# Turning the output projection of an attention kernel round, so that it yields the transposed result by seven block products

## The chip, the core and the metric

The kernel runs on one core of a Trainium2 chip. The core has a matrix engine (TensorE, "PE" in the profile, its weight loads "PEld"), a vector engine (VectorE, "DVE"), an engine for functions of one operand (ScalarE, "ACT"), a general engine (GpSimd, "POOL") and a queue processor (SyncE, "SP") that issues most of the DMAs. TensorE writes to PSUM, eight banks of 512 float32 values in each of 128 partitions; everything else lives in SBUF or in DRAM. The metric is device time in microseconds; the median of several runs counts. A profile is one further execution with its own time.

## What is computed

Eight images of 32 x 32 pixels with 256 channels pass through two attention layers, in float32.

```python
# layer 0: four heads, no mask; n = 1024 pixels, C = 256
q, k, v = split(x @ W_qkv)                  # per head, each n x 256
p   = softmax(q @ k.T * C**-0.5)            # n x n
res = concat_heads(p @ v)                   # n x 1024
x1  = res @ W_out + b_out + x
# layer 1: one head, 32 channels for f and g
f, g, h = x1 @ Wf + bf, x1 @ Wg + bg, x1 @ Wh + bh
y = gamma * (softmax(g @ f.T) @ h) + x1     # the output
```

Layer 0 has nearly all of the work: 32 pairs of image and head, each with two 1024 x 1024 x 256 products, against one narrow and one wide product an image in layer 1.

## The kernel before

**Folding.** For each head the kernel first forms `wqk`, the product of the query weights and the transposed key weights, and `wvo`, the product of the value weights and this head's rows of `W_out`. Scores then need only x and one projected q, and the values are x itself: `y` = x^T p, unnormalised, is projected by `wvo` at the end. x is held in rows (`rows`, pixels on the partitions) and transposed (`xT`, channels on the partitions).

**Seven products.** Most matrix products of layer 0 are cut into 2 x 2 blocks and done by seven block products instead of eight. `sum_a` and `sum_b` form the four sums of blocks that each side needs, on VectorE; `seven` runs the products in three thirds, `one`, `two` and `three`, into three PSUM banks x, y and z, and forms the four result blocks by a copy on ScalarE (`e`, and block 11) and five additions on VectorE (`u`, `v`, 22, 21, 12). The queries, the scores and `y` are made so. The projection is not: `project` does four matmuls of 128 x 128 by 128 x 256 for two groups of 128 rows (`po`, line 637), with `y` as the stationary side, and adds each group to the accumulated rows `rows1` by one VectorE instruction (line 648) that multiplies by the inverse of the softmax sum, a column with one value a row.

**Steps.** The program is a list of steps, each one block of 512 columns (`blk` 0 or 1) of one head of one image; for every image after the first, the two blocks of layer 1 of the image before stand between the heads (after head 1, for the last image after head 3). A step runs the scores of its own block, the products `y` of the block one step earlier (`one`), and the projection of the block two steps earlier (`two`). The last third of `y` runs into the next step.

**Order.** Within a step `put` gives every task a place from 0 to 10, and tasks are issued by place. TensorE, VectorE and ScalarE work strictly in this order (`manual_schedule`); a task that waits holds up what stands behind it on its engine. SP and GpSimd take theirs as the program gives it. Two pools of PSUM banks serve all: `ps` with 6 banks, for scores and `y`, and `psm` with 2, for the projection, the values of layer 1 and f and g.

**The sums of p.** `sums` forms the block sums of p for `y` and, from them, the sums over rows (`keys`): a wide add, two narrower ones, a reduction over partitions on GpSimd (line 593), a DMA of the row to DRAM (`line`) and one back as a column of four per partition (`st`). `invert` takes the inverses.

**Layer 1.** x1 has to be transposed. `turn_rows` does it without TensorE: DMAs move 32 x 32 squares to their place (line 377) and `nc.vector.transpose` turns each square (lines 382, 385). For x1 the squares go through the f-and-g tile. The last image's x1 is transposed on TensorE (`transpose_rows`) in the last step. `values` projects h by row groups into `v` (one `psm` bank a task, evacuated at line 729), `queries_apart` makes f and g; layer 1's product with p is `row_products`, which adds to `rows1` and leads to the output.

Buffers that the change touches: `rows` has 4, `xT` 2; `m0`, `rs`, `rb` one each.

Of the kernel before, what the change touches and what calls it, by code (L numbers as in the profile page):

```python
# [16 lines left out]
P = 128  # L17
# [3 lines left out]
def kernel(  # L21
# [14 lines left out]
):  # L36

# [111 lines left out]
    bout_sb = const.tile([P, C], F32, tag="bout", name="bout_sb")  # L149
# [8 lines left out]
    def load_rest():  # L158
        with nc.allow_non_contiguous_dma(reason="small bias vectors, loaded once"):
            nc.sync.dma_start(bout_sb, b_out.partition_broadcast(P))  # L160
# [20 lines left out]
    wblocks = {}  # L181
# [52 lines left out]
    def seven(name, width, parts, matmuls, outs, tags, copy, after=None):  # L234
# [7 lines left out]
        def bank(k):  # L242
            banks[k] = tile_of("ps", [P, NB], f"ps{k}_{name}")[:, :width]
# [22 lines left out]
        def one():  # L266
            for k, number in (("x", 1), ("y", 6), ("z", 5)):
                bank(k)
                product(k, number, True)
            nc.scalar.copy(scratch("e"), banks["x"])  # L270
            add(shaped(scratch("u")), "y", sbs["e"])
# [19 lines left out]
    NARROW = dict(e="eh", u="uh", v="w")  # L291

    def fold_weights(h):
# [20 lines left out]
        def multiply(i, what):  # L314
# [13 lines left out]
            if i == 0:  # L328
# [4 lines left out]
                wblocks[h] = b_operands(blocks, sums)  # L333

# [22 lines left out]
    def turn_rows(b, src, dst, layer, scratch=None):  # L357

        Q = 32

        def end():
            if b not in dst:
                dst[b] = tile_of("xT", [P, CC, N], f"x{layer}T_{b}")
            return dst[b]

        def flat(t):
            return t.rearrange("p u n -> p (u n)").rearrange("p (s q) -> p s q", q=P)  # L370

        def move(a, c=None):
            to, rows_v = flat(end() if scratch is None else scratch()), flat(src[b])
            if c is not None:
                to, rows_v = to[:, ts(c, NT), :], rows_v[:, c::CC, :]
            for q in range(P // Q):
                nc.sync.dma_start(to[ts(q, Q), :, ts(a, Q)], rows_v[ts(a, Q), :, ts(q, Q)])

        def piece(k, c):
            to = end()[:, c, ts(k, NB)]  # L380
            if scratch is None:
                nc.vector.transpose(to, to)
            else:
                squares = scratch()[:, k, :].rearrange("p (t c q) -> p t c q", c=CC, q=P)
                nc.vector.transpose(to.rearrange("p (t q) -> p t q", q=P), squares[:, :, c, :])

        return (
            [partial(move, a, c) for a in range(P // Q)
             for c in ((None,) if scratch else range(CC))],
            [partial(piece, k, c) for k in range(NBLK) for c in range(CC)],  # L390
        )

# [32 lines left out]
    def residual(b):  # L425


        def piece(i):
            if i == 0:
                rows1[b] = tile_of("rows", [P, NT, C], f"x1_{b}")  # L430
            nc.vector.tensor_tensor(
                rows1[b][:, ts(i, 2), :], rows[b][:, ts(i, 2), :],
                bout_sb.unsqueeze(1).broadcast_to([P, 2, C]), ALU.add,
            )

        return [partial(piece, i) for i in range(NT // 2)]
# [40 lines left out]
    def values_tile(name):  # L477
        v = tile_of("v", [P, NT, CV], name)
        nc.gpsimd.memset(v[:, :, C : C + 1], 1.0)
        return v  # L480


    class Layer0:
        def __init__(self, b, h):
            self.b, self.h, self.name = b, h, f"{b}_{h}"
            self.p, self.y, self.r = {}, {}, {}
            self.products_of, self.pblocks = {}, {}
# [8 lines left out]
        def queries(self):  # L496
# [6 lines left out]
            def after():  # L503
                t = tile_of("qs", [P, 3, NBLK, HB], f"qs_{self.name}")
                q = self.q.rearrange("p c (k e i) -> p c e k i", k=NBLK, e=2)
                blocks = [q[:, c, e] for c in range(CC) for e in range(2)]
                sums = [blocks[1]] + [t[:, k] for k in range(3)]
                self.pieces = sum_b(sums, *blocks)
                self.blocks = b_operands(blocks, sums)

            def piece(k):
                self.pieces[k]()  # L512

# [7 lines left out]
                WIDE, nc.scalar.copy, after,  # L521
            ), [partial(piece, k) for k in range(4)]

        def scores(self, blk):
# [10 lines left out]
            for g in range(0, half, 2):  # L535
# [3 lines left out]
                def after(g=g, out=out):  # L539
# [8 lines left out]
                         self.blocks[number][:, blk, :])  # L548
# [10 lines left out]
        def sums(self, blk):  # L559
# [6 lines left out]
            def start():  # L566
# [4 lines left out]
                s2 = tile_of("s2", [P, half, HB], f"s2_{n}")  # L571
                s3 = tile_of("s3", [P, half, HB], f"s3_{n}")
                sums = [t[:, 1], s2, s3, t[:, 0]]
# [8 lines left out]
            def first():  # L582
                t = made["t"]
                made["m"] = m = tile_of("m0", [P, 2, 2, HB], f"m_{n}")
                tt(m, t[:, :, 0:2, :], t[:, :, 2:4, :], ALU.add)

            def second():
                m = made["m"]
                r = tile_of("rs", [P, 2, HB], f"rs_{n}")
                tt(r, m[:, :, 0, :], m[:, :, 1, :], ALU.add)  # L590
                tt(r[:, 0, :], r[:, 0, :], r[:, 1, :], ALU.add)  # L591
                t = tile_of("rb", [P, NB], f"rb_{n}")
# [9 lines left out]
            return [partial(piece, i) for i in range(4)], [first, second]  # L602

        def invert(self, blk):
            n = self.first + blk * HT
            nc.vector.reciprocal(inverse[:, n : n + HT], self.r[blk])
# [22 lines left out]
        def project(self, blk):  # L629

            b = self.b
# [501 lines left out]
```

## Time and profile before

| | |
|---|---|
| Time, median of 3 runs | 2338.89 us (2338.29 to 2339.77) |
| The profiled execution | 2338.61 us; its span on the core 2336.7 us |
| Granted TensorE clock | 0.999 |
| VectorE, ScalarE, GpSimd busy | 1481.7, 522.5, 211.5 us |
| `po` matmuls | 1024 instructions, 128 x 128 by 128 x 256 |
| DMA | 42.94 MB, mean 18 GB/s; 158160 of 170257 packets under 512 B |

A row of a group reads: line, engine, operation, output tile <- input tiles, shapes, count | busy time in us, mean ns of one | idle time of the engine just before them, and who ended it. A float32 matmul shows as two instructions. A line of the timeline reads: start in us, length in us, engine, line, what it is, how many were merged, and in brackets the idle time of the engine before it with what ended it. A line of waits reads: who waited for whom, us in total, times, longest.

VectorE's longest rows in one ordinary step are the sums over 128 x 1024 elements (1.21 us each), the additions from PSUM of 128 x 512 (0.69 us) and of 128 x 256 (0.42 us). The reduction over partitions takes GpSimd 3.2 us a block. In the tail, the last step begins at 2248.8 us with the last third of `y` of block 0, and the span ends at 2336.7 with the last rows of layer 1 of the last image.

### The profile page before, as it was taken

Reading aid. Unit: us, or ns where it says so; the run is one execution under the profiler, and the core shown is the slowest. Engines: PE = TensorE matmul, PEld = TensorE weight load, DVE = VectorE, ACT = ScalarE, POOL = GpSimd, SP = SyncE. Lnnn points to the kernel's source line nnn. Section 1 sums busy time; section 2 is a strip of 40 time slices with the busy share of each in tenths; the row PEclk is TensorE's granted clock in tenths of the full one; section 3 lists DMA queues with packets and bytes.
Section 4 is the critical chain, followed back from the end, with each engine's and each line's share of the span. In section 5 each row is a group of like instructions: output and inputs, shape, how many; then the busy total and the mean of one; then the engine's idle time right before and its main releaser. Section 6 shows DMA issues by size and latency. Waiting matters only on the chain.

```text
span 2336.7 us, 26026 instructions
## 1 busy us (share of the span) xinstructions
PE 2326.9 (100%) x10394; PEld 1918.8 (82%) x10394; DVE 1481.7 (63%) x2398; ACT 522.5 (22%) x875; POOL 211.5 (9%) x79
## 2 busy tenths in 40 slices
PE   9999999999999999999999999999999999999999
PEld 7888888788878888788887888878888788888877
DVE  6667775377754767557774577645776457766635
ACT  2222222222221222212222122221222222222222
POOL 0111111011110111101111011110011101101110
PEclk9999999999999999999999999999999999999999
DMA  4000010100101001110011000110001100000100
GB/s 138 1 1 1 1 37 14 34 1 11 27 17 32 1 19 21 19 29 1 19 26 18 24 1 19 30 18 19 1 19 30 19 19 1 1 1 1 30 7 31
DMA packets 170257, 42.94 MB, mean 18 GB/s; under 512 B 158160, under 2 KB 163024, under 8 KB 170128
## 3 DMA queue, kind: packets, MB, share of 16 engines
q1 hardware_dynamic: 170128, 41.20, 8.0%
q8 instruction: 84, 1.38, 0.3%
q14 instruction: 45, 0.37, 0.1%
HBM read 13.37 MB, written 8.52 MB: 9 GB/s over the span
## 4 chain that ended last, share of the span: by engine, by line
PE 99%; DVE 1%; DMA 0%; issue 0%; ACT 0%
PE psy_y L247 14%; PE psy L247 14%; PE psx L247 9%; PE pa_l L834 9%; PE po L637 9%; PE psx_y L247 9%; PE psz_y L247 9%; PE psz L247 9%; PE psy_q L247 4%; PE psx_q L247 2%; PE psz_q L247 2%; PE pr_v_l L466 2%; PE ps_l L746 1%; PE pm_fg L703 1%; PE pwqk L318 0%; PE pwvo L318 0%
## 5 line engine op out<-in xcount | busy, mean ns | idle before, releaser
L593 POOL PARTITION_ALL_REDUCE rb<-rs x64 | 206.9, 3233 | 2046.6 <-DVE rs L591 2019.8
L247 PE MATMUL psx<-q,x0T 128*128 128x256 f32 x1024 | 263.6, 380 | 0.0
L247 PE MATMUL psy<-qs,xs 128*128 128x256 f32 x1024 | 263.0, 379 | 0.0
L247 PE MATMUL psz<-q,xs 128*128 128x256 f32 x1024 | 262.8, 379 | 0.0
L541 ACT ACTIVATE p<-p 128x1024 f32<-128x1024 f32 x128 | 135.3, 1057 | 554.8 <-DVE p L264 554.8
L247 PE MATMUL psy_y<-s,xt 128*128 128x256 f32 x1024 | 242.4, 380 | 0.1
L637 PE MATMUL po<-wvo,y 128*128 128x256 f32 x1024 | 241.9, 379 | 0.0
L247 PE MATMUL psx_y<-p,x 128*128 128x256 f32 x1024 | 241.9, 379 | 0.0
L834 PE MATMUL pa_l<-v_l,s_l 128*128 128x257 f32 x1024 | 232.1, 381 | 0.4 <-DVE v_l L729 0.4
L247 PEld LDWEIGHTS psx<-q,x0T 128*128 128x128 f32 x1024 | 194.0, 190 | 45.2 <-issue 21.0
L637 PEld LDWEIGHTS po<-wvo,y 128*128 128x128 f32 x1024 | 194.6, 190 | 39.5 <-issue 14.8
L834 PEld LDWEIGHTS pa_l<-v_l,s_l 128*128 128x128 f32 x1024 | 193.8, 190 | 36.6 <-issue 10.5
L247 PEld LDWEIGHTS psx_y<-p,x 128*128 128x128 f32 x1024 | 194.7, 190 | 34.0 <-issue 8.6
L247 PEld LDWEIGHTS psy_y<-s,xt 128*128 128x128 f32 x1024 | 191.9, 190 | 30.6 <-issue 2.4
L247 PEld LDWEIGHTS psy<-qs,xs 128*128 128x128 f32 x1024 | 194.5, 190 | 27.0 <-DVE qs L512 0.4
L247 PEld LDWEIGHTS psz<-q,xs 128*128 128x128 f32 x1024 | 194.7, 190 | 26.3
L264 DVE TENSOR_TENSOR u<-psy,e 128x512 f32<-128x512 f32 x128 | 88.4, 691 | 144.3 <-ACT e L270 73.4
L276 ACT ACTIVATE p<-psx 128x512 f32<-128x512 f32 x128 | 76.4, 597 | 413.7 <-PE psx L247 413.6
L264 DVE TENSOR_TENSOR v<-psy,e 128x512 f32<-128x512 f32 x128 | 87.8, 686 | 124.5 <-PE psy L247 124.5
L247 PE MATMUL psy<-qs,x0T 128*128 128x256 f32 x512 | 131.6, 380 | 0.7 <-DVE v L264 0.7
L648 DVE SCALAR_TENSOR_TENSOR x<-po,inverse,x 128x256 f32<-128x256 f32 x256 | 111.9, 478 | 31.3 <-PE po L637 22.4
L270 ACT COPY e<-psx 128x512 f32<-128x512 f32 x128 | 73.8, 576 | 257.8 <-PE psx L247 257.8
(120 smaller groups left out, 2839.8 us busy)
## 6 DMA issues: line engine op xcount, KB each, us to landing
out_dram<-x SPq DMA_DIRECT2D x15, 512.0 KB, 2.6
x<-in_x_dram SPq DMA_DIRECT2D x14, 512.0 KB, 4.6
x0T<-x SPq DMA_DIRECT2D x224, 32.0 KB, 1.9
fg<-x SPq DMA_DIRECT2D x112, 64.0 KB, 2.1
fg<-fg SPq DMA_DIRECT2D x56, 64.0 KB, 2.0
w<-in_L_conv_W_qkv_dram SPq DMA_DIRECT2D x4, 512.0 KB, 7.3
x<-in_x_dram SPq DMA_DIRECT2D x4, 256.0 KB, 4.8
w<-in_L_conv_W_qkv_dram SPq DMA_DIRECT2D x4, 256.0 KB, 6.4
```

Of the source, the lines that this page charges most:

```text
L247: nc.tensor.matmul(banks[k][:, ts(i, w)], lhsT=lhsT, rhs=rhs, start=first and n == 0, stop=True, skip_group_check=True,)
L264: nc.vector.tensor_tensor(dst, shaped(banks[k]), shaped(other), ALU.add)
L270: nc.scalar.copy(scratch("e"), banks["x"])
L276: copy(outs["11"](), shaped(banks["x"]))
L466: nc.tensor.matmul(pm[:, ts(j, C)], lhsT=src()[:, c, ts(2 * t2 + j, P)], rhs=w()[:, c, :], start=(c == 0), stop=(c == CC - 1),)
L541: exp(both, both)
L593: nc.gpsimd.partition_all_reduce(t, r.rearrange("p e i -> p (e i)"), P, bass_isa.ReduceOp.add)
L637: nc.tensor.matmul(pm[:, ts(j, C)], lhsT=self.y[blk][:, c, ts(2 * t2 + j, P)], rhs=folded[self.h][1][:, c, :], start=(c == 0), stop=(c == ...
L648: nc.vector.scalar_tensor_tensor(acc, pm[:, ts(j, C)], inverse[:, n : n + 1], acc, ALU.mult, ALU.add)
L703: nc.tensor.matmul(pm[ts(k, half)], lhsT=w[:, c, :], rhs=x1T_of[b][:, c, ts(k, NB)], start=(c == 0), stop=(c == CC - 1),)
L746: nc.tensor.matmul(pm, lhsT=self.f[ts(r, CK), ts(j0 + r, P)], rhs=self.g[ts(r, CK), ts(blk, NB)], start=True, stop=True,)
L834: nc.tensor.matmul(pm[:, : C + 1], lhsT=p[:, j, ts(ti, P)], rhs=v[:, j, : C + 1], start=(j == 0), stop=(j == NT - 1),)
```

## The change

The projection is turned round. With `wvo` stationary and `y` moving, it gives the transposed contribution, channels on the partitions, and it runs through `seven`: the four sums of `wvo` are formed once a head (`oblocks`), those of `y` in every step (`yt`). It takes two PSUM banks of the `psm` pool, since y and z share one (`two_banks`). The result `o` (in the `m0` buffer) now needs one inverse per column: the inverses, after `invert`, are written to DRAM as a row and spread to all partitions (`invb`) by two DMAs, and one VectorE instruction multiplies a step later; for the last block the inverse is taken of the reduced row itself (`invert_all`). GpSimd then issues a DMA that adds `o` to `x1T` in SBUF. `x1T` starts as x^T plus the bias (`residual`, now on ScalarE, in step 1 of the image). Layer 1 reads `x1T` directly; the rows of x1, needed for the output, come from turning `x1T` back (`turn_back`), for the last image too, so no transposition on TensorE is left there.

Around it: the sums of q are made for one block at a time; the sums of p share storage (one in place of a block of p, one in place of another sum) and their row sums are added row by row; the intermediate of f and g lies in the values' tile, which is taken earlier; x of the next image is loaded and turned one head earlier; `rows` gets 3 buffers and `xT` 3.

```diff
-    def seven(name, width, parts, matmuls, outs, tags, copy, after=None):
+    def seven(name, width, parts, matmuls, outs, tags, copy, after=None, two_banks=False):
@@
+            if not two_banks:
+                banks[k] = tile_of("ps", [P, NB], f"ps{k}_{name}")[:, :width]
+            elif k == "z":
+                banks[k] = banks["y z"][:, width : 2 * width]
+            else:
+                t = tile_of("psm", [P, NB], f"ps{k}_{name}")
+                banks["y z"], banks[k] = t, t[:, :width]
@@ fold_weights
+                t4 = const.tile([P, 4, P], F32, tag=f"wo{h}", name=f"wo{h}")
+                sums = [t4[:, k, :] for k in range(4)]
+                blocks = [t[:, c, ts(e, P)] for e in range(CC) for c in range(CC)]
+                run(sum_a(sums, *blocks))
+                oblocks[h] = a_operands(blocks, sums)
@@ residual
-            nc.vector.tensor_tensor(
-                rows1[b][:, ts(i, 2), :], rows[b][:, ts(i, 2), :],
-                bout_sb.unsqueeze(1).broadcast_to([P, 2, C]), ALU.add,
+            nc.scalar.activation(
+                x1T_of[b][:, c, :], xT_of[b][:, c, :], AF.Identity, bias=boutT_sb[:, c : c + 1]
             )
@@ sums
-                sums = [t[:, 1], s2, s3, t[:, 0]]
+                sums = [t[:, 1], t[:, 0], blocks[2], t[:, 0]]
@@
-                tt(m, t[:, :, 0:2, :], t[:, :, 2:4, :], ALU.add)
+                tt(r, t[:, :, 0, :] if k == 1 else r, t[:, :, k, :], ALU.add)
@@ invert
+            line = tile_of("line", [1, NB], f"inv_{self.name}_{blk}")
+                nc.sync.dma_start(line.rearrange("o (t p) -> p (o t)", p=P), inv)
+            self.rb[blk] = t = tile_of("invb", [P, NB], f"invb_{self.name}_{blk}")
+            nc.sync.dma_start(t, line[0].partition_broadcast(P))
@@ project
-                        nc.tensor.matmul(
-                            pm[:, ts(j, C)],
-                            lhsT=self.y[blk][:, c, ts(2 * t2 + j, P)],
-                            rhs=folded[self.h][1][:, c, :],
-                    nc.vector.scalar_tensor_tensor(
-                        acc, pm[:, ts(j, C)], inverse[:, n : n + 1], acc, ALU.mult, ALU.add
-                    )
+                    y = self.y[blk]
+                    t = tile_of("yt", [P, 3, HB], f"yt_{n}")
+                    blocks = [y[:, c, ts(e, HB)] for c in range(CC) for e in range(2)]
+                    sums = [blocks[1]] + [t[:, k] for k in range(3)]
+                    made["l"] = sum_b(sums, *blocks)
+                    made["b"] = b_operands(blocks, sums)
...
+            def add():
+                o = made["o"]
+                nc.vector.tensor_tensor(
+                    o, o, self.rb[blk].unsqueeze(1).broadcast_to([P, CC, NB]), ALU.mult
+                )
+                nc.gpsimd.dma_start(
+                    x1T_of[self.b][:, :, ts(blk, NB)], o, accum_op=ALU.add
+                )
+            return [partial(piece, i) for i in range(4)], seven(
+                f"o_{n}", HB, 1,
+                lambda number: [(0, oblocks[self.h][number], made["b"][number])],
...
+                LAST, nc.scalar.copy, two_banks=True,
+            ), [add]
@@ the steps
-            put(u.project(k), *((3, 7) if l0 else (2, 6) if blk == 0 else (3, 7)))
+            ysums, tasks, adds[i] = u.project(k)
+            put(ysums, *((1.1, 1.2, 1.3, 3.3) if l0 else (2.6, 2.7, 2.8, 3.1) if blk == 0 else
+                         (1.1, 1.2, 1.3, 2.1)))
+            put(tasks, *((3, 5.5, 7) if l0 else (5.2, 6, 7.2) if blk == 0 else
+                         (3, 5, 7) if nxt else (2.1, 4.1, 4.6)))
+        if i - 1 in adds:
+            put(adds[i - 1], 0.5)
@@
-                moves, turned = turn_rows(a.b - 1, rows1, x1T_of, 1, step(i + 2)[0].fg_tile)
-                put(moves, 0.1, 0.2, 0.3, 0.4)
-                put(turned, 5.4, 6.4, 7.2, 7.4)
+                moves, turned1 = turn_back(a.b - 1)
+                put(moves, 3, 4, 5, 6, 7, 8, 8.9, 9.3)
@@
         if not l0 and blk == 0:
             put(a.values(), 0.9, 1, 3, 5, 8)
+            put(turned1, 2.5, 2.9, 4.2, 5.1)
         if nxt is None:
-            put(transpose_rows(B - 1, rows1, x1T_of, 1), 2.5, 4.5, 8.1, 8.2)
-            put(final.queries(), 2.4, 6.5, 9)
+            fg = final.queries()
+            moves, turned1 = turn_back(B - 1)
+            put(moves, *[9.1 + 0.1 * k for k in range(8)])
@@
-    run(own[:1], s0[:1], prod[:1], p0[:1], s0[1:], prod[1:2], p0[1:2])
-    weave((prod[2:] + own[1:], 0, 1), (s1, 0.3, 0.7), (p1[:2], 0.55, 0.95), (p0[2:], 0.1, 0.9))
+    run(own[:1], prod[:1], fg, s0[:1], p0[:1], prod[1:2], s0[1:], p0[1:2])
+    weave((prod[2:] + own[1:], 0, 1), (s1, 0.3, 0.7), (p1[:2], 0.55, 0.95), (p0[2:], 0.1, 0.9), (turned1, 0.3, 1))
```

## The prediction

> **What bounds the kernel now.** I read the page first (busy shares, the chain of waits, the costliest groups), then TensorE's own waits, then the timeline of three stretches: an ordinary step of layer 0, a step with layer 1 in it, and the tail.
>
> ```profile
> PE 2326.9 (100%) x10394; PEld 1918.8 (82%) x10394; DVE 1481.7 (63%) x2398; ACT 522.5 (22%) x875; POOL 211.5 (9%) x79
> PE 99%; DVE 1%; DMA 0%; issue 0%; ACT 0%
> L637 PE MATMUL po<-wvo,y 128*128 128x256 f32 x1024 | 241.9, 379 | 0.0
> L648 DVE SCALAR_TENSOR_TENSOR x<-po,inverse,x 128x256 f32<-128x256 f32 x256 | 111.9, 478 | 31.3 <-PE po L637 22.4
> ...
> PE psy L247 <- DVE v L264: 0.7, 2, 0.3
> PE pa_l L834 <- DVE v_l L729: 0.4, 1, 0.4
> ```
>
> TensorE is the chain: 99% of it, and its waits on VectorE over the whole span are 0.7 and 0.4 us. So every matmul removed is time removed, and every wait newly put on TensorE is time added; nothing else counts. The stretch below, steps of head 0 of one image, gives the pitch and the room:
>
> ```profile
> 1121.47:1149.10 27.63, 27.63 (x130) 24.27 (x128) 19.66 (x32) 6.04 (x10) 3.41 (x3) 1.00 0.01 1
> 1149.10:1182.60 33.50, 33.50 (x143) 26.89 (x142) 25.10 (x41) 7.21 (x12) 2.98 (x2) 1.00 0.10 32
> ...
> 1129.24 1.89 PE L637 MATMUL po<-wvo,y 128*128 128x256 f32 x8
> 1130.97 1.03 PE L247 MATMUL psy<-qs,x0T 128*128 128x256 f32 x4
> 1131.83 1.03 PE L247 MATMUL psz<-q,xs 128*128 128x256 f32 x4
> ```
>
> The columns after the stretch are its length and the busy time of PE, PEld, DVE, ACT and POOL. Eight `po` instructions start 1.73 us before their successor, so one takes 0.216 us, not the 379 ns of its row, which overlap. VectorE has 8.0 and 8.4 us free in these steps, but it works in a fixed order, so where its work stands matters as much as how much there is.
>
> **What the Trainium skill says.** "Perfetto Trace Analysis", section Identifying the Most-Contended Engine: matmul busy time is a poor measure, weight-load busy a better one. Here PE shows 100% and PEld 82%; since TensorE's waits are about 1 us, I take the pitch as the bound all the same. "DMA: Bandwidth & Descriptors", section SWDGE vs HWDGE vs iDMA: accumulating during a DMA is possible only from GpSimd's queue; no run here has one. The same page, Anatomy of one DMA, prices such a DMA at 2.0 us plus bytes over 436 GB/s; the trace has only SP's transfers of 512 KB, which land in 2.6 us (output) and 4.6 us (loads). "SBUF — State Buffer", section Who interferes with whom: VectorE with two SBUF inputs contends with GpSimd's reads, not its writes, so making descriptors beside the sums should not be held; no trace here shows it.
>
> **The change part by part.**
> *TensorE, removed.* The projection of a block goes from 8 products of 256 columns to 7; each is two instructions. 64 blocks x 2 x 0.216 = 27.6 us. The 16 transposes of x1 in the last step go as well: four take 0.43 us (2263.85 to 2264.28), so 1.7 us. Together 29.3.
>
> *VectorE, added.* Per block: four sums of y (0.42 each, as L591) 1.7; five adds from PSUM (0.42, as `u_y`) 2.1; one multiplication of 128x1024 (as L580) 1.21; minus four of L648 at 0.478, 1.9. That is +3.1, times 64 = 199 us. Sums of q by block: 256 x 0.42 instead of 128 x 0.685, +20. Sums of p row by row: 3 x 0.685 + 0.425 instead of 1.215 + 0.68 + 0.425, +10. Sums of wvo 16 x 0.29 = 5, a further turned image 3; the residual (21) moves to ScalarE. VectorE comes to about 1698 us, 73%. ScalarE gets 64 x (0.357 + 0.372) + 16 x 1.06 = 64 us, reaching 25%. Totals bind nothing; order might.
>
> *Ordinary steps, hidden.* I laid out an even step of layer 0 by these durations: TensorE 27.2 us, VectorE 23.2 us. The tight points are where TensorE needs a sum: the third sum of y is ready 7.8 us into the step, wanted at 8.2; the second sum of p at 12.1, wanted at 12.5; the last add of the step ends about 1 us into the next, where the PSUM bank is wanted 1.7 us in. So nothing is lost, with 0.3 to 0.7 us to spare; if VectorE were 0.5 us later, about 0.2 us would be lost at some 45 such steps. The odd steps (33.1 us) have a little more room; head 0's, with the sums of x, is even.
>
> *Inverses and accumulation, hidden.* The row of sums takes 3.2 us on GpSimd and about 4 us through the two small DMAs; the inverse then goes to DRAM and back to all partitions, two more at about 2 us each, wanted a step (27 us) later. Ahead of it on SP stand at worst four turning DMAs of 0.69 us. The product is scaled by 4.3 us into the step after; GpSimd then issues the 512 KB accumulation. By the skill's price that is 3.2 us, an estimate; doubled for reading the destination, 6. The next user of its one buffer (`m0`) is ScalarE's copy 16.4 us into the step, so 12 us are free. Below it costs nothing, above it ScalarE's exponentials queue behind the copy and TensorE's banks behind them. I take 3 to 6.
>
> *Steps with layer 1, added.* The first third of the projection now stands right behind a values task and needs two `psm` banks; one is the bank that task has just filled. The fourth values task of one such step, and its evacuation:
>
> ```profile
> 969.32 1.89 PE L466 MATMUL pr_v_l<-wh_sb,x1T 128*128 128x256 f32 x8
> 971.04 1.89 PE L637 MATMUL po<-wvo,y 128*128 128x256 f32 x8
> ...
> 971.25 0.75 DVE L729 SCALAR_TENSOR_TENSOR v_l<-pr_v_l,gamma_sb,bh_sb 128x512 f32<-128x512 f32 x1 [1.83 <-PE pr_v_l L466]
> ```
>
> The bank is free at 972.0; the second product would start at 971.04 + 0.43 = 971.5. That is 0.55 us; the next third follows at once and waits about 0.25 for the add that reads the same bank. 0.8 x 7 images = 5.6 us. Were the evacuation queued behind one sum of p (1.2), 14; none stands there.
>
> *Tail, added.* x1 of the last image is no longer transposed on TensorE but turned by 32 DMAs and four transposes of VectorE (0.70 each) placed among the last values tasks.
>
> ```profile
> 986.77 17.16 SPq L377 DMA_DIRECT2D x0T<-x  x25
> ...
> 2305.44 0.74 DVE L729 SCALAR_TENSOR_TENSOR v_l<-pr_v_l,gamma_sb,bh_sb 128x512 f32<-128x512 f32 x1
> 2306.34 25.37 PE L834 MATMUL pa_l<-v_l,s_l 128*128 128x257 f32 x116 [0.39 <-DVE v_l L729]
> ```
>
> One DMA takes SP 17.16/25 = 0.69 us, all 32 take 22, plus 2 to land. They start once the output of the block before is written, 23 us after that step began, so end near 47; VectorE arrives at the first transpose near 45.5 and stops for about 2. Behind it stand the evacuations of the values, which already today end late enough to hold TensorE 0.39 us. The four transposes put the last of them 2.9 us later, the re-placed maxima of p add about 1: 4.1 us, or 6.3 with the stop. I take 5.3. The f and g matmuls of the last image are there before and after; their evacuation holds the first scores 0.4 us. With the two thirds placed side by side in the last step (0.6) that is 1 us more; the head of the kernel and the first image, whose turned x meets full steps, get 1.0.
>
> *Sum.* The profiled execution took 2338.61 us (its span is 2336.7, 1.9 around it), 0.3 under the median of 2338.89. 2338.6 - 29.3 + 5.6 + 5.3 + 1.0 + 1.0 = 2322.2.
>
> **The rivals.**
> *All hidden, 2311 us.* VectorE runs ahead more than I laid out, and the tail's DMAs land first: 2338.6 - 29.3 + 2 (half of what the last values task costs). For it: TensorE waited 1 us in all before. Against it: the bank wait with layer 1 is plain from the order.
> *Given back in the steps, 2335 us, no change.* VectorE is half a microsecond later than I laid out in the ordinary steps: 45 x 0.3 = 13.5 on top of 2322. For it: 85% busy (23.2 of 27.2) in a fixed order with less than 0.5 us to spare at two points. Against it: at the third product of y VectorE must wait for TensorE every step, so lateness does not pile up.
> *Slower: the accumulating DMA, 2370 us.* One buffer holds the scaled product until the accumulation has landed. If landing takes d us, some 50 steps lose d - 12. At 12.5 the kernel is slower than before by over 0.2%, since 2322 + 50 x 0.45 passes 2343.6; at 13 it takes 2370 or so. For it: no accumulating DMA in the trace, and in head 1 and 2 the turning DMAs with their 128-byte pieces share the 16 engines (28% busy at most today). Against it: the priced 3.2 us would have to be off fourfold.
> *The change does not do what it says:* if the sums left the bounds, the general path behind the flag would run, far above every number here; I count it with slower.
>
> **How the numbers follow.** Forecast 0.55; all hidden 0.22; given back 0.10; slower 0.13. 0.2% is 4.7 us, about what a measurement can tell from no change: faster below 2334.2, slower above 2343.6. Faster: the first two and a third of the third, 0.80. No change: the rest of the third, 0.07. Slower 0.13. The range goes from all hidden with nothing at the tail (2309) to the third case (2336); it leaves out the slow case and some 4% more. The forecast's own bounds are 2316 (0.55 a layer-1 step, tail 4.1, nothing else) to 2329.
>
> **What would show it.** Right: instructions on PE fall by 144; DVE busy near 1698; waits on PE for `v_l` of (or banks it filled) some 0.5 us in each of seven layer-1 steps and some 5 in the tail, none for `yt` or `ss`. The accumulations leave GpSimd within 5 us of a step's start and ScalarE's copy into `o` never waits for a DMA. Wrong: PE waiting on ACT or on DVE in ordinary steps; a wait of ScalarE on the accumulation; a lower granted clock. If it comes out near 2310, I priced the bank waits and the tail too high; above 2336, the accumulation or VectorE's order.

## The result and the profile after

The changed kernel takes 2352.71 us (median of 6 runs, 2348.16 to 2357.54) where the kernel before takes 2338.92 (2338.09 to 2339.77) beside it: a ratio of 1.0062, with an interval of 1.0048 to 1.0076. It is slower, and 30 us above the forecast of 2322. The profiled execution took 2352.15 us, its span 2350.3, its granted clock 0.996.

The page of the changed kernel, with busy times, the chain of waits, one group of matmuls, one group of GpSimd and two DMA issues (the last number is us to landing):

```profile
PE 2313.2 (98%) x10250; PEld 1897.2 (81%) x10250; DVE 1657.0 (71%) x2963; ACT 584.8 (25%) x1015; POOL 289.5 (12%) x143
...
PE 77%; DMA 7%; SPq 6%; issue 5%; DVE 3%; POOL 1%; ACT 0%; DVEq 0%; POOLq 0%
...
L255 PE MATMUL psy_y<-ss,xt 128*128 128x256 f32 x512 | 127.0, 393 | 15.5 <-DVE ss L612 15.4
...
L702 POOL DMA_DIRECT2D x1T<-o x64 | 77.9, 1217 | 433.7 <-DVE o L699 316.6
...
x1T<-o POOLq DMA_DIRECT2D x64, 512.0 KB, 5.0
invb<-inv SPq DMA_DIRECT2D x63, 256.0 KB, 4.9
```

TensorE is no longer 99% of the chain; transfers, SP and VectorE have come into it. The instructions of PE fell by 10394 - 10250 = 144, as reckoned. The new waits, from the same kernel's view of waits (waiter, releaser, us in total, times, longest):

```profile
PE psy_y L255 <- DVE ss L612: 15.4, 6, 4.1
PE pa_l L899 <- DVE v_l L794: 3.3, 1, 3.3
PE psy L255 <- DVE v L272: 3.0, 6, 0.9
PE psy_o L255 <- DVE v_l L794: 2.9, 7, 0.4
...
DVE o L699 <- DMA invb<-inv: 33.3, 7, 7.1
DVE x0T L394 <- DMA x0T<-x: 19.5, 6, 3.7
...
SPq L648 <- DMA inv<-inverse: 500.1, 63, 10.5
```

The largest wait of TensorE is for a sum of p, but the sum is only the messenger. VectorE works in a fixed order, and ahead of that sum stands the multiplication of the projection by the inverses (L699), which waits for `invb`. `invb` is spread by SP's second transfer (L648), which cannot start before the first has landed: SP stands there 500 us in all 63 blocks. One such step on the timeline, from the turned sums to TensorE's wait:

```profile
650.25 0.17 DVE L641 RECIPROCAL inverse<-st 128x4 f32<-128x4 f32 x1
...
660.88 0.52 SPq L646 DMA_DIRECT2D inv<-inverse  x1
...
669.38 0.33 SPq L648 DMA_DIRECT2D invb<-inv  x1
...
674.05 1.22 DVE L699 TENSOR_TENSOR o<-o,invb 128x1024 f32<-128x1024 f32 x1 [4.76 <-DMA invb<-inv]
...
675.19 1.22 DVE L612 TENSOR_TENSOR ss<-p 128x1024 f32<-128x1024 f32 x1
...
678.35 1.97 PE L255 MATMUL psy_y<-ss,xt 128*128 128x256 f32 x8 [1.81 <-DVE ss L612]
```

The inverse is ready at 650.4. Its first transfer leaves at 660.9, because SP issues 16 moves of f and g first (649.5 to 660.8, some 0.6 us each), and the second leaves 8.5 us later. VectorE has come to the multiplication at 669.3, 18.9 us after the inverse; it stands 4.8 us and TensorE 1.8. This happens in six of the seven first steps with layer 1. In the six, moves that turn `x1T` back keep SP busy until the moves of f and g begin, between 1.4 us before the inverse is ready and 1.2 after. In the seventh they are over earlier, the moves of f and g begin 5.6 us before the inverse (2212.5 against 2218.1), and VectorE waits 0.2 us.

After a longer wait TensorE also runs slowly. Two neighbouring windows behind the wait of 4.10 us of another image (length, then busy time and count of PE, PEld, DVE, ACT, POOL; then granted clock, DMA share, GB/s):

```profile
1258.40:1262.00 3.60, 3.19 (x8) 2.60 (x9) 3.57 (x9) 0.00 (x0) 0.00 (x0) 0.50 0.84 128
1262.00:1266.00 4.00, 4.00 (x16) 3.38 (x15) 2.18 (x4) 0.00 (x0) 0.00 (x0) 0.79 0.00 0
```

The clock granted is 0.50 of full speed: eight matmuls take 3.6 us there, not 1.73. Four stretches of this kind lie in the six steps, of 3.4, 3.4, 6.8 and 3.4 us. They begin before the wait has ended in two cases, and 2.4 us of them pass while TensorE stands anyway; half of the rest, 7.3 us, is lost.

In ordinary steps all went as planned. Two starts of the q product, one head (two blocks) apart:

```profile
521.19 1.02 PE L255 MATMUL psx_q<-x0T,wqk 128*128 128x512 f32 x2
...
581.59 1.02 PE L255 MATMUL psx_q<-x0T,wqk 128*128 128x512 f32 x2
```

The same two starts of the kernel before are at 519.72 and 580.98. The head shrank from 61.26 to 60.40 us, by 0.86, which is 4 x 0.216: the two products fewer. The distances between such starts, over six images, give the place of the loss; the column without the round trip (the inverse's way to DRAM and back) is the second experiment:

| From one q product to the next | before | after | without the round trip |
|---|---|---|---|
| an ordinary head | 61.26 | 60.40 | 60.40 |
| the head with layer 1 behind it, mean of six | 119.24 | 122.63 | 118.62 |
| the next head, with the turned x | 48.51 | 48.81 | 48.07 |

### The profile page after: what moved, and what is told of

It reads as the page before. It is cut to its first block, busy times and chain, and to the rows that moved or that the text cites. A ratio compares the mean times of both kernels' runs of the same rounds, so it can differ in the third digit from the quotient of the medians.

```text
span 2350.3 us, 27210 instructions
## 1 busy us (share of the span) xinstructions
PE 2313.2 (98%) x10250; PEld 1897.2 (81%) x10250; DVE 1657.0 (71%) x2963; ACT 584.8 (25%) x1015; POOL 289.5 (12%) x143
## 4 chain that ended last, share of the span: by engine, by line
PE 77%; DMA 7%; SPq 6%; issue 5%; DVE 3%; POOL 1%; ACT 0%; DVEq 0%; POOLq 0%
PE psy L255 13%; PE psy_y L255 12%; PE psz L255 9%; PE psx L255 8%; PE psz_y L255 8%; PE psx_y L255 8%; DMA inv<-inverse 5%; PE psy_o L255 5%; PE pa_l L899 4%; SPq L386 3%; PE psy_q L255 3%; PE psx_q L255 2%; PE psz_q L255 2%; PE psx_o L255 2%; SPq L382 1%
## 5 line engine op out<-in xcount | busy, mean ns | idle before, releaser
L255 PE MATMUL psy_y<-p,xt 128*128 128x256 f32 x1024 | 241.9, 379 | 0.0
L255 PEld LDWEIGHTS psy_y<-p,xt 128*128 128x128 f32 x1024 | 194.6, 190 | 26.4
L255 PE MATMUL psy_y<-ss,xt 128*128 128x256 f32 x512 | 127.0, 393 | 15.5 <-DVE ss L612 15.4
L702 POOL DMA_DIRECT2D x1T<-o x64 | 77.9, 1217 | 433.7 <-DVE o L699 316.6
L255 PEld LDWEIGHTS psy_y<-ss,xt 128*128 128x128 f32 x512 | 99.3, 196 | 34.0 <-issue 18.5
L255 PE MATMUL psz_y<-ss,xt 128*128 128x256 f32 x512 | 123.2, 384 | 0.0
```

The lines of the kernel that those rows point to most:

```text
L255: nc.tensor.matmul(banks[k][:, ts(i, w)], lhsT=lhsT, rhs=rhs, start=first and n == 0, stop=True, skip_group_check=True,)
L702: nc.gpsimd.dma_start(x1T_of[self.b][:, :, ts(blk, NB)], o, accum_op=ALU.add)
```

## The experiments

The first theory was: the inverse's way to DRAM and back, waiting on SP behind f and g, costs all of it. The rivals were VectorE's larger load in the steps with layer 1, and a lower clock from another cause.

**One: the two transfers apart, f and g behind the first.**

```diff
@@ invert
+            self.line[blk] = line
+        def spread(self, blk):
+            ...
             nc.sync.dma_start(t, line[0].partition_broadcast(P))
@@ the steps
+            put([partial(u.spread, k)], 5.0)
-                put(moves, 1.6, 1.7, 1.8, 1.9)
+                put(moves, 3.5, 3.6, 3.7, 3.8)
```

> The inverse's row is written as before, but the DMA that spreads it is issued by a task of its own at place 5, and the 16 f-and-g moves stand between the two instead of ahead of both. Theory 1 (the inverses come late because SP holds their two DMAs behind the moves and then stands 8.6 us for the first to land; VectorE stops at the scaling, and TensorE after it, which also halves its clock for some us): the 33 us that VectorE waits for invb go, TensorE's waits of 15.4 us for the sums of p go, no half-clock stretch is left but the one at the end: 2352 less 15.4, 8.5 and some of the 3.8 for the late turned x, so 2324 to 2329. Theory 2 (VectorE simply has too much to do in the steps with layer 1; the DMA wait only stands where it would be late anyway): the waits of TensorE in these steps stay within a third, 2345 or more.

Measured: 2333.11 us (2331.81 to 2337.31), ratio 0.9976 [0.9965, 0.9988]. The waits for the sum fell from 15.4 to 0.4 us, but the time stayed above the 2324 to 2329 that the theory named. Two waits of TensorE and VectorE, from the profiled execution, which is the slowest of the seven:

```profile
PE psy L255 <- DVE v L272: 8.5, 7, 3.4
...
DVE x0T L394 <- DMA x0T<-x: 24.9, 6, 6.2
```

Here the next head waits, for the turned x of the following image: the later second transfer holds SP at another place, and nine moves of x stood behind it (432.4 to 438.8 us, after `invb` had left at 432.1). So SP's order, and not only the inverse's own lateness, is part of the loss.

**Two: no round trip.** The multiplication uses a constant tile and both transfers are left out.

```diff
@@ invert
-            line = ...
-            nc.sync.dma_start(t, line[0].partition_broadcast(P))
+            if blk not in self.rb:
+                self.rb[blk] = fixed
```

> Leaves out the scaling by the inverses' row: both DMAs of the round trip are gone and VectorE multiplies by a fixed tile of 1/1024 instead, with the same instruction in the same place. Theory 1: the whole price of the round trip goes, as in the split or up to 3 us better, 2322 to 2328. Theory 2: VectorE's work is unchanged, so 2345 or more.

Measured: 2324.84 us (2323.91 to 2325.18), ratio 0.9939 [0.9922, 0.9955]. The waits for the sum are gone, and so are those for the turned x. All of VectorE's other new work and the accumulating DMAs are still there, so these two rivals fall. The round trip costs 2352.7 - 2324.8 = 27.9 us. By the table, 6 x (122.63 - 118.62) = 24.0 of it lies in the steps with layer 1 and 6 x (48.81 - 48.07) = 4.4 in the head that follows. The 24.0 are 16.3 for the six waits and 7.7 behind them, nearly all of it at half clock. (The waits count 16.3 by the starts of the same matmuls in both runs, 15.4 by the view: it measures each from the modelled end of the matmul before, which makes it 0.16 us shorter.) The parts make 28.4. That this is so near to 27.9 is partly chance: in the profiled executions, 27.4 apart, the changed kernel also loses 1.4 us at its head, before the first scores, and the second experiment loses 2.9 in the tail by a half clock that the changed kernel doesn't have there.

**Three: stalls of set length in the kernel before**, two to eight extra additions of 1.2 us on VectorE ahead of the sums, one more in each image.

```diff
+            if not l0 and blk == 0:
+                def extra(p):
+                    t = tile_of("m0", [P, 2, NB], f"extra_{a.name}")
+                    for _ in range(a.b + 2):
+                        nc.vector.tensor_tensor(t, p[:, 0:2, :], p[:, 0:2, :], ALU.add)
+                put([partial(extra, u.p[k])], 0.7)
```

> The kernel before, with 2 to 8 more VectorE additions of 128x1024 (unused results) ahead of the sums of p in the seven steps with layer 1, one more for each image: 2.4 to 9.7 us more of VectorE work, of which the first 2.5 us or so are free. It measures what a wait of TensorE costs. If a wait costs only its own length, the granted clock stays at 1 throughout and the time rises by the sum of the waits, about 0+1+2+3+5+6+7 = 24 us. If a wait beyond some length also halves the granted clock for a while, as in four places of the changed kernel, then the longer steps show stretches at 0.5 of 3.4 us and more, and the time rises by 10 us more than the waits.

Measured: 2366.65 us in a single run, with the kernel before at 2338.68 beside it: 28.0 more. TensorE's waits:

```profile
PE pr_v_l L466 <- DVE v_l L729: 19.9, 6, 6.5
```

Windows over the steps with waits of 1.4, 2.7, 4.0, 5.2 and 6.5 us, in this order (the granted clock is the third number from the end):

```profile
960.00:975.00 15.00, 13.57 (x66) 11.02 (x65) 10.25 (x14) 3.18 (x7) 0.00 (x0) 1.00 0.01 1
1250.00:1265.00 15.00, 12.31 (x61) 9.89 (x60) 10.25 (x14) 2.44 (x5) 0.00 (x0) 1.00 0.00 0
1540.00:1555.00 15.00, 11.05 (x47) 8.45 (x46) 10.00 (x13) 2.44 (x5) 0.00 (x0) 0.89 0.00 0
1835.00:1850.00 15.00, 10.19 (x38) 8.67 (x39) 9.09 (x12) 2.05 (x5) 0.00 (x0) 0.77 0.00 0
2250.00:2270.00 20.00, 13.53 (x54) 10.46 (x53) 12.42 (x15) 2.44 (x5) 0.00 (x0) 0.74 0.00 1
```

The half clock needs none of the changed kernel's DMAs; a wait of TensorE brings it. The stretches are 3.4, 6.8 and 10.2 us long at the last three. Of these 20.5 us, 7.1 lie within the waits themselves; half of the rest is 6.7. The rise beyond the waits is 28.0 - 19.9 = 8.1, of which the 0.16 us that the view leaves out of each wait make about 1.

**Four: only the order on SP.** One line, f and g behind the inversion; the transfers stay together.

```diff
-                put(moves, 1.6, 1.7, 1.8, 1.9)
+                put(moves, 3.5, 3.6, 3.7, 3.8)
```

> The changed kernel with one edit: the 16 moves of f and g are placed behind the inversion of the step (3.5 to 3.8 instead of 1.6 to 1.9); the two transfers of the inverse stay together on SP. If the order on SP is the cause (some 10 us of f and g moves ahead of the inverse), the inverse leaves some 10 us earlier in the six steps, the waits of psy_y for ss fall from 15.4 us to under 1, the half clock behind them goes too, and the time falls by 22 to 26 us to 2326 to 2331; TensorE's waits in the head-2 steps (for the sums v, behind the late turned x) stay as they are. If the slow transfers alone are the cause (8.6 and 4.9 us, whoever stands ahead), the ss waits stay above 5 us and the time above 2340.

Measured: 2364.76 us (2360.17 to 2371.34), ratio 1.0118 [1.0099, 1.0137]: slower still, and the time that the first theory named is missed by over 30 us, although its waits did fall as it said, from 15.4 to 0.2. SP's queue in one of the steps, and TensorE's wait there:

```profile
1237.54 1.24 SPq L646 DMA_DIRECT2D inv<-inverse  x1
1238.83 0.51 SPq L781 DMA_DIRECT2D fg<-v_l  x1
1239.39 0.59 SPq L782 DMA_DIRECT2D fg<-v_l  x1
1240.02 0.59 SPq L781 DMA_DIRECT2D fg<-v_l  x1
1247.40 0.34 SPq L648 DMA_DIRECT2D invb<-inv  x1
1247.79 0.51 SPq L782 DMA_DIRECT2D fg<-v_l  x1
```

```profile
1253.21 1.09 PE L811 MATMUL ps_l<-fg 32*128 32x512 f32 x2 [3.84 <-DMA fg<-v_l]
```

The second transfer comes to SP's head at 1240.6 and waits until 1247.4 for the first to land; the last moves of f and g stand behind it, and the scores of layer 1 wait for them. In six waits these scores lose 12.9 us (7.7 put down to the moves, 5.2 to no one in the view), and four half-clock stretches follow. Here the order alone only chose who waits. The first transfer takes some 9 us here too (from its issue to that of the second, median of 63), SP stands still through them, and someone has to pay for it.

**Five: the inverse without transfers.** The sums stand on all partitions after GpSimd's reduction, and ScalarE makes exp(-ln(sum)).

```diff
-            line = ...
-            nc.sync.dma_start(t, line[0].partition_broadcast(P))
+            if blk not in self.rb:
+                self.rb[blk] = t = tile_of("invb", [P, NB], f"invb_{self.name}_{blk}")
+                nc.scalar.activation(t, self.total[blk], AF.Ln)
+                nc.scalar.activation(t, t, AF.Exp, scale=-1.0)
```

> The changed kernel with the inverse's way through DRAM replaced: the sums of p already stand on all partitions after GpSimd's all-reduce, so ScalarE writes exp(-ln(sum)) of 128x512 in two instructions (0.6 us each) in the inversion's place; nothing else is changed. If the round trip on SP is the whole loss, the result is that of leaving it out (2324.8 us): 2323 to 2328, the o multiplication waits for no DMA, ss waits under 1 us, the turned x not late. If ScalarE's order matters instead (the ln waits for the all-reduce and ScalarE's copies and exponentials queue behind it, or the tables for ln and exp alternate at 1.28 us a load, 2.6 us a step), TensorE waits on ScalarE in ordinary steps and the time is above 2335.

Measured: 2325.05 us (2324.84 to 2325.38), ratio 0.9939 [0.9923, 0.9956], the time of the second experiment. ScalarE's tables do alternate, and its groups show what that costs:

```profile
L644 ACT ACT_TABLE_LOAD x63 | 80.8, 1283 | 1.1
L645 ACT ACT_TABLE_LOAD x63 | 80.8, 1283 | 1.1
L645 ACT ACTIVATE invb<-invb 128x512 f32<-128x512 f32 x63 | 39.7, 630 | 0.7
L644 ACT ACTIVATE invb<-rb 128x512 f32<-128x512 f32 x63 | 39.7, 630 | 0.7
```

That is 241 us more on ScalarE, and no new wait of TensorE: an engine at 25% had room for it.

**Six and seven: the two other costs, each alone on top of the fifth.** The four transposes behind the values of the tail; and the third values task of a layer-1 step away from the projection.

```diff
@@ six
-    weave((prod[2:] + own[1:], 0, 1), (s1, 0.3, 0.7), (p1[:2], 0.55, 0.95), (p0[2:], 0.1, 0.9), (turned1, 0.3, 1))
-    weave((final.products(0), 0, 1), (p1[2:], 0, 0.9), ([judge, decide], 0.9, 1))
+    weave((prod[2:] + own[1:], 0, 1), (s1, 0.3, 0.7), (p1[:2], 0.55, 0.95), (p0[2:], 0.1, 0.9))
+    weave((turned1, 0, 0.1), (final.products(0), 0, 1), (p1[2:], 0, 0.9), ([judge, decide], 0.9, 1))
@@ seven
-            put(a.values(), 0.9, 1, 3, 5, 8)
+            put(a.values(), 0.9, 1, 3, 3.9, 8)
```

> The kernel with exp(-ln(sum)) (e5_log, 2325.05 us) with one more edit: the four transposes of the turned x1 of the last image stand ahead of the last products of block 0 instead of among the last values tasks. VectorE is busy without a gap from 2277.5 us there, so the last values are ready 4 x 0.63 = 2.5 us earlier. If the tail's loss is these transposes, the wait of pa_l for v_l falls from 3.3 us to about 0.8, the stretch at half clock behind it (6.8 us, 3.4 lost) goes as well since stalls of up to 1.8 us brought none, and the time falls by 5 to 6.5 us to 2318.5 to 2320. If the re-placed maxima of p hold the values, the wait stays above 2.5 us and the time above 2322.

> e5_log with one more edit: in the steps with layer 1 the values task at 5 stands at 3.9, so that other products lie between it and the projection's first third at 5.2. If the wait for the bank that the values task has just filled is the loss (0.58 and 0.32 us, seven times, 6.3 us), both gaps go and the time falls by 5 to 6.5 us to 2318.5 to 2320. If the bank is held by VectorE's order (the add that reads it is queued behind sums of p), only the first gap goes or neither, and the time stays above 2321.

Measured: 2319.31 us (2319.21 to 2319.66), ratio 0.9916 [0.9903, 0.993], and 2319.37 us (2318.63 to 2320.39), ratio 0.9918 [0.9904, 0.9931]: each 5.7 us less. In the first, the wait for `v_l` fell from 3.3 to 0.4 us and the half clock went. In the second, the wait of `psy_o` for `v_l` (2.9 us in seven times) is gone. Of the gap of 0.58 and that of 0.32 us at each such projection the first went and the second stayed: it is the wait for the add that reads the bank, 1.1 us in all by the view of waits. In the profiled executions, 6.2 us apart, the seven steps brought 0.68 each, 4.8 together; the rest comes from a shorter stretch at half clock in the tail (3.4 instead of 6.8 us, behind the same wait of 3.3), which the edit doesn't touch.

**Eight: both, and the last block's inverse by exp(-ln) as well.**

```diff
-            if nxt is None:
-                put([partial(u.invert_all, k)], 0.6)
```

> e5_log with both edits of e6_tail and e7_psm, and in the last step the inverse by exp(-ln) too instead of VectorE's reciprocal of 128x512 (3.35 us ahead of the last projection, about 1.8 us of waits). If the three losses are independent, the gains add up: 2325.05 - 6 - 6 - 1.5, 2310 to 2313. If VectorE's order makes one of the waits come back elsewhere, 2315 or more.

Measured: 2315.11 us (2314.95 to 2315.63), ratio 0.9899 [0.9884, 0.9914]. That is 9.9 us less than the fifth, where 13.5 were expected. The seventh's share is only the 4.8 us of the banks, since the sixth takes the half clock of the tail as a whole; and the last edit brought 0.3 us, not 1.5: the wait for `yt` fell from 0.7 to 0.4, and TensorE's wait of 1.0 us for an add did not move. The long reciprocal was not its cause. The timeline of this run shows what is:

```profile
2239.68 0.59 PE L255 MATMUL psy_o<-yt,wo 128*128 128x256 f32 x2
2240.31 0.42 DVE L272 TENSOR_TENSOR v_o<-psy_o,e_o 128x256 f32<-128x256 f32 x1 [0.18 <-PE psy_o L255]
2240.77 0.42 DVE L272 TENSOR_TENSOR o<-psy_o,v_o 128x256 f32<-128x256 f32 x1
2241.25 0.70 PE L255 MATMUL psy_o<-yt,wvo 128*128 128x256 f32 x2 [0.98 <-DVE o L272]
```

In the last step the last two thirds of the projection stand with nothing between them on TensorE, and the third writes the bank that these two adds have just read. 5.7 + 4.8 + 0.3 makes 10.8, 0.9 more than measured; in the profiled executions 0.5 of that lies behind the last matmul (from its end to the end of the span the sixth takes 5.4 us and the eighth 5.9).

**Nine and eleven: what makes 8.6 us?** The row of inverses is written in pieces of four bytes, 512 of them. It is written in pieces of 16 and of 8 bytes.

```diff
@@ nine
-                nc.sync.dma_start(line.rearrange("o (t p) -> p (o t)", p=P), inv)
+                nc.sync.dma_start(line.rearrange("o (p t) -> p (o t)", p=P), inv)
@@ eleven
+                nc.sync.dma_start(
+                    line.rearrange("o (a p u) -> p (o a) u", p=P, u=2),
+                    inv.rearrange("p (a u) -> p a u", u=2),
+                )
```

> The changed kernel with the inverse written to DRAM in its own order, four neighbours of a partition together: 128 pieces of 16 bytes instead of 512 of 4 (the scaling then meets the wrong columns; the amount of work is the same). If the number of pieces makes the 8.6 us (2.1 us fixed, as the reading of the same row in 4-byte pieces lands, and 6.5 us for 512 pieces, 12.7 ns each), the first transfer lands in about 3.7 us, the spreading starts 5 us earlier, the six ss waits (4.1 us at most) go, and the time falls to 2325 to 2332. If it is the write to DRAM itself, whatever its pieces, it stays over 8 us and the time stays at 2348 to 2356.

> The changed kernel with the inverse written in 256 pieces of 8 bytes (the scaling meets the wrong columns; the amount of work is the same). If the landing grows with the pieces, 128 in 1.6 us and 512 in 8.6, it lies on the line between, 1.6 + 128 x 0.018 = 3.9 us, and the ss waits are gone or nearly: 2323 to 2330. If only pieces of 4 bytes are slow, 1.6 to 2.2 us; if anything under 16 is, 8 us and the time of the change.

Measured: 2323.27 us (2321.96 to 2325.83), ratio 0.9937 [0.992, 0.9954], and for the eleventh 2325.78 in a single run. The DMA views of the changed kernel, of the pieces of 8 and of those of 16 bytes, in this order (us to landing last):

```profile
st<-line SPq DMA_DIRECT2D x64, 2.0 KB, 2.1
inv<-inverse SPq DMA_DIRECT2D x63, 2.0 KB, 8.6
```

```profile
inv<-inverse SPq DMA_DIRECT2D x63, 2.0 KB, 4.1
```

```profile
inv<-inverse SPq DMA_DIRECT2D x63, 2.0 KB, 1.6
```

These landings are medians of the few transfers whose landing the trace tells, 3 in the changed kernel and 6 in the other two. SP's own waits for the first transfer cover nearly all of them; in the eleventh and the ninth they are these, where the changed kernel has 500.1:

```profile
SPq L651 <- DMA inv<-inverse: 149.2, 60, 3.8
SPq L648 <- DMA inv<-inverse: 62.2, 50, 2.2
```

From the issue of the first transfer to that of the second, which waits for it, pass 8.6, 3.1 and 1.6 us at the median of all 63. So the time falls with the pieces, by 5.5 us for the first 256 fewer and by 1.5 for the next 128: 21 and 12 ns a piece, not on one line as the eleventh expected. The packet records of the first transfer end 1.3, 1.1 and 1.0 us after its issue, so the difference arises behind them, where no view reaches. Reading the same row from DRAM in 512 pieces takes 2.1 us, so it is the writing of small pieces to DRAM that is dear. Their number, their length and their order in DRAM change together here; which of these counts is not shown. In both runs TensorE's waits for the sum are gone.

**Ten: the complete kernel with this cure.** Reading and writing the row in the same order keeps every sum with its column; the edits of six and seven are added.

```diff
-                    nc.sync.dma_start(st, line.rearrange("o (t p) -> p (o t)", p=P))
+                    nc.sync.dma_start(st, line.rearrange("o (p t) -> p (o t)", p=P))
-                nc.sync.dma_start(line.rearrange("o (t p) -> p (o t)", p=P), inv)
+                nc.sync.dma_start(line.rearrange("o (p t) -> p (o t)", p=P), inv)
```

> The changed kernel, complete, with the sums read from the row and the inverses written to it in the same order, four neighbours to a partition (16-byte pieces; nothing is permuted, since both ends agree), the values task at 3.9 and the four transposes of the tail behind the values. From e9_pieces (2323.27 us) the bank waits take 4.8 us and the tail 3.3 to 5.8: 2312.5 to 2315.5, level with e8_all (2315.11) or a little below, without the extra work on ScalarE. If the inverses' DMAs, though short, still hold SP's moves once the waits elsewhere are gone, 2317 or more.

Measured: 2314.60 us (2313.90 to 2315.49), ratio 0.9896 [0.988, 0.9913]: 24.6 us below the kernel before and 38 below the change as it came. From its page, and the one wait of TensorE that is left in the steps with layer 1:

```profile
PE 2299.5 (99%) x10250; PEld 1892.7 (82%) x10250; DVE 1657.7 (72%) x2963; ACT 584.9 (25%) x1015; POOL 289.6 (13%) x143
```

```profile
PE psy_o L255 <- DVE u_o L272: 1.1, 7, 0.2
```

## Why the prediction was wrong

The failed step is "Inverses and accumulation, hidden", in its first half. It priced the inverse's two transfers at "about 2 us each", put before them "at worst four turning DMAs of 0.69 us", and had the result "wanted a step (27 us) later". All three are wrong. The trace has 8.6 and 4.9 us for the transfers, and ahead of them 16 moves of f and g (11 us), which the prediction did not place in SP's order. And VectorE comes to the multiplication 18.9 us after the inverse in these steps. From a ready inverse to the multiplication 24 us pass there, where the prediction's prices make 7. The price of 2 us fits the nearest row in the trace of before (`st<-line`, 2.1 us), but that row is read from DRAM, and this one is written to it in four-byte pieces. "The Trainium skill", page "DMA: Bandwidth & Descriptors", section Specifications, says that transfers below 512 bytes are done by read-modify-write; this bears on it, and the prediction did not use it. The runs agree that a small write can be dear. But all three lengths of piece, 4, 8 and 16 bytes, lie below 512, and they took 8.6, 3.1 and 1.6 us; that read-modify-write is what takes the time, no run here shows.

In the ordinary heads the same transfers are hidden, and nothing was lost. The prediction was right there with less room than it thought: the multiplication comes 17 to 20 us after the inverse, and the second transfer leaves 8 to 12 us after it and takes 5 to land. Of the 20 us that it counted on (27 less 7), some 6 were left at best.

The other steps, against the runs:

- *TensorE, 29.3 us less.* Right: 144 instructions fewer, 0.86 us a head.
- *VectorE and ScalarE.* 1657 us against 1698 reckoned, 585 against 587. Right in kind: their totals bind nothing.
- *Ordinary steps hidden.* Right, to 0.01 us a head.
- *The accumulation.* Right: 5.0 us to landing where 3 to 6 were taken, and ScalarE's copy into `o` never waits for it. So the mechanism of the slower rival did not occur. A time above 2336 was to point to it or to VectorE's order; it came from SP's queue, and VectorE's order only passed it on.
- *Steps with layer 1, 5.6 us.* The seventh experiment shows 4.8 and a rest of some 0.3 us an image, 6.3 by the gaps. Right.
- *Tail, 5.3 us.* The sixth shows 5.7. The size is right by luck, the make-up is not: the wait is 3.3 us, 2.9 more than before. VectorE stopped for the transfers 1.1 us in the changed kernel and not at all in the fifth, and the wait was the same in both. The rest is the half clock that follows in some runs and in others not.
- *Last step 1.0.* The waits for `o` and `yt` are 1.0 and 0.7. The first is that of the two thirds placed side by side, for which 0.6 was taken.
- *The turned x.* Not in the sum at all. Its moves stand on SP behind the same standing transfer, 4.4 us.

With the failed step taken out the sum holds: 2322.2 predicted, 2324.8 measured without the round trip, about 2.9 of these by the half clock in the tail. What was wrong in it is one term of nothing that should have been 28: 16.3 for the waits, 7.7 behind them and 4.4 for the turned x. The working has three small slips besides, which change nothing: the forecast's lower bound comes out at 2317.3, not 2316; the case given back in the steps takes 0.3 us a step where the layout had put 0.2; and 2.9 and 1 in the tail make 3.9, not 4.1.

What stays open: what the first transfer does in the 7 us behind its last packet record, and the 0.4 us of the eighth experiment that are left.

## What to carry to other kernels

Where a step sends work through a queue, write that queue's whole order in the step out, with every transfer that the code puts there, and ask for each one that waits who stands behind it; moving them about made others wait, so that it gave back only 19.6 of the 27.9 us in the first experiment and lost 12 more in the fourth. Price a small transfer by one of the same direction and in the same pieces, not by its bytes: 2 KB took 1.6 or 8.6 us here. The cheapest cure may be to let both ends agree on an order with longer pieces. Reckon, too, how long after the producer the consumer is really reached: a step of slack was 17 to 20 us here and not 27. A stall of TensorE may cost more than its length, since half the clock can follow it.

## What the runs showed of the hardware that was not expected

The half clock after a stall. "The Trainium skill", page "TensorE: Matmul & The Clock Gate", Part 1, describes a clock halved after an idle window of about 3.4 us, and windows that run freely. The traces agree with the length and with the free running. All stretches that slow the kernel are of 3.4 us or two or three times that, and those of one run lie on one grid. By the clock records of the traces they begin at 389.84, 966.69, 1256.83 and 1837.09 us in the changed kernel, which is 169.0, 85.0 and 170.0 times 3.413 us apart, and at 1546.98, 1837.11 and 2253.54 in the third experiment, 85.0 and 122.0 times.

So what counts is not the length of a wait but how much of it falls into one window. These are three neighbouring windows of the changed kernel's grid at its wait of 2.3 us, and two at its wait of 3.3 us in the tail, which ends one window and begins the next:

```profile
386.43:389.84 3.41, 1.16 (x6) 0.93 (x6) 3.41 (x7) 0.37 (x1) 1.09 (x1) 1.00 0.58 100
389.84:393.25 3.41, 3.41 (x10) 2.66 (x9) 3.38 (x7) 0.00 (x0) 0.00 (x0) 0.50 0.41 54
393.25:396.66 3.41, 3.12 (x15) 2.41 (x13) 1.64 (x5) 0.25 (x1) 0.00 (x0) 1.00 0.00 0
...
2314.96:2318.37 3.41, 1.57 (x7) 0.86 (x5) 3.34 (x5) 0.22 (x1) 0.00 (x0) 1.00 0.00 0
2318.37:2321.78 3.41, 1.98 (x9) 1.80 (x10) 2.65 (x6) 0.08 (x1) 1.78 (x1) 1.00 0.00 0
```

PE is busy for 1.16 us in the first, and the next is at half clock. With 1.57 and 1.98 us none follows. The wait of 2.7 us in the third experiment is cut in the same way (1.95 and 2.19 us busy, none), and a window with 1.22 us there brings one. In all runs but the fourth, 1.4 us of busy time or less in a window at full clock was followed by a window at half clock, and 1.5 us or more was not; so the window need not be idle as a whole. In the fourth, two waits of 1.9 and 1.6 us brought one each, beside the narrow matmuls of layer 1's scores (32 x 128 stationary), with 1.5 and 1.8 us busy. Busy time is therefore not all that counts, and what else does is not shown.

Where the boundary falls differs from run to run. The same wait of 3.2 to 3.3 us in the tail brought no such window in the changed kernel, one in the first and seventh experiments and two in the fifth. It would also fit the changed kernel's wide spread of 9 us between runs, against 1.7 of the kernel before, which has no such wait.
